# A fused relation layer with residual, one NeuronCore: one tile instead of four keeps its bias in the PSUM bank, and a new hand-written order of work

## Chip, cores, metric

One core of one Trainium2 chip. The metric is the device time of one execution in microseconds, the median of several executions; times inside an execution come from one profiled execution and count from the start of its span.

## Reference

For each of 4 sequences of 1024 rows with 512 columns, and a conditioning vector of 256 numbers per sequence (float32 throughout):

```python
hidden = jnp.concatenate([hidden0, hidden1], axis=-1)      # both are cond_512
x_mean = jnp.mean(x, axis=1, keepdims=True)
fused = jnp.concatenate([x, x_mean * ones_L, hidden[:, None, :] * ones_L], axis=-1)
relation = jax.nn.relu(jnp.einsum('bld,do->blo', fused, W) + b)
return x + relation
```

W is 1536 x 512. Its first 512 rows meet x, row by row; the rest gives one bias vector per sequence.

## The kernel before

**Work.** The 4096 rows are 32 tiles of 128 rows (8 per sequence). A tile's product is x (128 x 512) by W0 (512 x 512), in four slices j of the inner dimension, each as three matmuls on halves of the numbers: `hi` is the value rounded to the matmul's format, `lo` the rest, so x W0 = hi w_hi + lo w_hi + hi w_lo (`product`, L351 to L365; n = 0, 1, 2 in that order). That is 12 matmuls of 512 columns per tile, 396 in all with tile 31 done in two halves of 256 columns, so that its second half alone is late at the end.

**Names.** `X` loads x by rows (for the final sum, and for tiles 0 and 1 as the source of the transposes), `Z` loads it a second time, in 32-row quarters, for VectorE's transposes. `W` loads the four slices of W0; `wh`, `wl` make `w_hi`, `w_lo` (L209 to L221). `y0`, `y1` gather tiles 0 and 1 into a column order that TensorE transposes (`T0`, `T1`, L260); all later units (tiles 2 and 3, then four tiles each) are transposed by VectorE (L262). `h` makes `hi` on ACT and the column sums for the mean (L269), `l` makes `lo` (L275). `p5.2` is a block: the three products of tile 5, slice 2; `p0.1.2` a single product; `p31.1r` the three half products of tile 31's right half. For each sequence r, `as`, `c`, `m`, `f`, `fa`, `vh`, `vl` build the bias in the PSUM tile `acc`, the matmul `pb` (L339) spreads it over the rows, `bc` copies it to SBUF (L343). The eight PSUM banks are five for outputs (tile t in bank t mod 5), two for transposes, one for `acc`.

**Three ways out of a bank** (`WAYS`, one letter per tile):

```python
if WAYS[t] == "K":  # K{t}: o <- bank, ACT L428 or DVE L426;  b{t}: o <- o + bias, L432
...
else:               # "B", K{t}: o <- bank + bias, DVE only
    nc.vector.tensor_tensor(o, bank(t), biases[r], ALU.add)            # L436
...
nc.scalar.activation(o, o, AF.Relu)                                    # r{t}, L443
...
nc_of[e].tensor_tensor(x_tile(t), o, x_tile(t), ALU.add)               # F{t}, L450
...
# "I", P{t}: bank <- bias ahead of the products (ACT); F{t}: x <- max(bank, 0) + x
nc.scalar.activation(bank(t), biases[r], AF.Copy)                      # L415
nc.vector.scalar_tensor_tensor(x_tile(t), bank(t), 0.0, x_tile(t), ALU.max, ALU.add)  # L419
```

Tile 31, the last, is always "I" in two halves (L395, L399). `S` stores a finished tile from the place where its x lay.

**Order.** Nothing is scheduled by the program: `ORDER`, a list of some 550 names, is walked once and each name issues its instructions (L452 to L457). A suffix picks the engine (`@d` VectorE, `@a` ScalarE, `@p` GpSimd). So the list sets each engine's queue, and the DMA queue too: all transfers but the first go through SP, one after the other, and a store waits there for the sum that it stores. Every engine works its queue strictly in order.

Of the kernel before, what the change touches and what calls it, by code (L numbers as in the profile page):

```python
# [19 lines left out]
ORDER = """
W0@a X0.0 fill X0.1 relu fill W1 fill W2 fill fill W3 fill Z2.0 y0.0@d fill y0.1@d y0.2@d Z2.3 fill wh0r@a Z2.1
wh0l@d T0.2 T0.1 wl0l@d fill Z2.2 T0.0 y1.0@a y1.1@d T0.3 wl0r@p Z3.3 T1.2 h0.2 T1.0 T1.3 h0.0 l0.2@d h0.1 Z3.0
wh1@d p0.0.2 l0.0@d T1.1 p0.1.0 h1.1 Z3.2 wh2@d p0.0.1 h1.0 l1.1@d h1.2 p0.2.0 wl1@d p1.0.2 wh3@a p1.0.0 l0.1@d
p1.1.0 Z3.1 h1.3 l1.0@d p0.0.0 wl3@d h0.3 p1.1.1 p0.2.1 p1.3.0 wl2@p l1.2@d p0.1.2 l1.3@d p1.0.1 l0.3@d Z4.2 p0.3.2
p1.1.2 p0.1.1 p1.3.1 T2.2 p1.2.1 T2.0 p0.2.2 Z4.1 h2.2 p0.3.1 h2.0 p1.3.2 l2.2@d p1.2.2 l2.0@d p2.2 T2.3 Z4.3 T2.1
p3.0 h2.1 p1.2.0 h2.3 p2.0 l2.1@p Z4.0 K1@a l2.3@d p0.3.0 p3.2 K0@d C p3.1 B p2.3 V T3.2 M2 p3.3 T3.1 h3.2 p2.1 M0
h3.1 l3.2@d p4.2 T3.3 l3.1@p K2@a p5.2 T3.0 M1 h3.3 K3@d p7.2 h3.0 l3.3@p p7.1 l3.0@d M3 p4.0 to0 p5.0 T4.3 Z5.2
Z5.1 T4.0 p6.2 h4.3 Z5.3 t2 p4.3 T4.2 l4.3@p p4.1 t3 h4.2 T4.1 p6.1 h4.0 as0 l4.0@d p7.3 K4@a ac1@p Z5.0 t1 p5.3 t0  # L30
l4.2@d p5.1 ac0@d p8.3 Z7.3 c0.0 K5@a h4.1 p9.2 c0.1 p9.0 l4.1@p Z6.1 m0.0 p6.3 m0.1 p9.1 Z6.3 m0.2 p8.0 m0.3 p6.0
Z6.2 p8.2 K6@a Z6.0 f0 p8.1 fa0 p10.1 T5.1 Z7.1 vh0 p11.3 h5.1 vl0 p11.2 K8@a T5.0 Z7.0 l5.1@p p11.0 T5.2 pb0 p7.0
T5.3 bc0@a as1 p11.1 b1@p Z8.2 h5.2 c1.0 p10.2 Z8.0 h5.0 p10.3 c1.1 b0@p h5.3 p10.0 l5.2@d K7@a Z7.2 to1 p9.3 l5.0@d
K10@a l5.3@p m1.0 r0@a p12.1 X3.1 K9@a X0.2 p12.0 m1.1 b2@p K11@a p12.2 m1.2 X2.0 X1.1 p13.1 m1.3 b4@p r2@a p13.0
r1@a T6.3 f1 p15.3 b3@p T6.1 h6.3 p14.0 T6.2 h6.1 fa1 F1@p p14.2 h6.2 T6.0 p15.1 vh1 l6.2@d l6.1@p S1 h6.0 p14.3
X1.0 T7.2 p13.2 Z9.2 vl1 l6.3@p h7.2 Z8.1 p15.2 l6.0@d p14.1 Z8.3 T7.1 b6@p pb1 T7.0 p13.3 bc1@a b7@p p12.3 r6@a K14
Z9.0 p16.3 T7.3 F0@p r7@a K12 p15.0 h7.0 l7.2@d p16.1 h7.3 F2@p K13 p19.1 as2 p17.3 S0 h7.1 c2.0 l7.3@p X5.1 p16.2
r3@a Z9.3 K15 p16.0 Z9.1 to2 c2.1 b5@p p19.0 m2.0 X2.1 p17.1 m2.1 l7.1@p p18.0 m2.2 p20.3 b8@p m2.3 p19.3 l7.0@d f2
p20.2 F3@p r4@a fa2 p17.2 T8.0 vh2 p19.2 F7@p S3 h8.0 vl2 p18.2 r5@a T8.3 p17.0 F4@p T8.1 h8.3 p18.3 l8.0@d F6@p pb2
p20.1 bc2@a h8.1 p18.1 K16 F5@p S6 r8@a p20.0 K17 r14@a p21.1 T8.2 b9@p S5 T9.0 X3.0 p22.2 h8.2 S7 K18 p22.0 l8.1@p  # L40
r9@a S2 K20 X5.0 as3 p21.0 S4 K19 r18@a F14@p p22.1 X4.1 l8.2@d h9.0 X6.0 p22.3 c3.0 F8@p p25.0 X7.1 T9.1 p21.2 X6.1
T9.2 l8.3@p p21.3 h9.2 p23.2 K21 F9@p p25.1 X7.0 T9.3 r21@a S8 p24.1 c3.1 h9.3 b10@p X4.0 p23.1 S14 l9.0@d h9.1
p26.2 r13@a to3 F21@d r20@a p25.2 b11@p K22 p23.3 m3.0 p25.3 l9.1@p r11@a m3.1 p27.3 r22@a m3.2 r12@a p27.2 F11@p
m3.3 p27.0 F20@d f3 p23.0 S11 F13@p r10@a S20 fa3 p24.3 S21 vh3 p24.0 S9 F10@p S13 vl3 p24.2 l9.2@d p26.3 F12@p K23
pb3 p26.1 bc3@a l9.3@p S12 r17@a p27.1 K24 S10 P28 p26.0 K25 r23@a p28.0 F22@d r24@a F23@d p28.1 S22 r15@a K27 P29
S23 p28.2 F15@p P30 p28.3 P31r F18@d r27@a p29.0 S15 F17@p r16@a F28 S18 p29.2 r19@a p30.3 r25@a F19@d S17 p29.1
F16@p K26 S19 S28 p31.1r r26@a p29.3 F27@d S16 P31l p31.3r F25@d S27 p31.0r F24@p F29 p31.2r S25 p30.2 F31r S29
p30.1 F26@p S24 S31r p31.2l p30.0 S26 p31.1l F30 p31.3l p31.0l S30 F31l S31l
""".split()


# [433 lines left out]
```

## Time and profile before

| what | before |
|---|---|
| three executions, us | 101.2, 101.21, 102.0 (median 101.21) |
| the profiled execution, us | 101.09 |
| its span, us | 99.3 |
| busy share: TensorE, VectorE, GpSimd, ScalarE | 94%, 82%, 68%, 57% |
| granted TensorE clock | 1.00 of full speed throughout |
| moved by DMA | 27.88 MB, 281 GB/s over the span |

A row of the timeline is: start, time from the first start to the last end of the merged instructions, engine, line, operation, what it writes and reads, count, and in brackets the idle time of that engine before it and what ended it. PE is TensorE, DVE VectorE, ACT ScalarE, POOL GpSimd, SP the engine that issues the transfers. Successive instructions of an engine overlap a little, and matmuls overlap by almost half their length. A tile name's running number is left out (po is any of the five output banks).

### The profile page before, as it was taken

Reading aid. Unit: us, or ns where it says so; the run is one execution under the profiler, and the core shown is the slowest. Engines: PE = TensorE matmul, PEld = TensorE weight load, DVE = VectorE, ACT = ScalarE, POOL = GpSimd, SP = SyncE. Lnnn points to the kernel's source line nnn. Section 1 sums busy time; section 2 is a strip of 40 time slices with the busy share of each in tenths; the row PEclk is TensorE's granted clock in tenths of the full one; section 3 lists DMA queues with packets and bytes.
Section 4 is the critical chain, followed back from the end, with each engine's and each line's share of the span. In section 5 each row is a group of like instructions: output and inputs, shape, how many; then the busy total and the mean of one; then the engine's idle time right before and its main releaser. Section 6 shows DMA issues by size and latency. Waiting matters only on the chain.

```text
span 99.3 us, 1422 instructions
## 1 busy us (share of the span) xinstructions
PE 93.6 (94%) x417; PEld 75.3 (76%) x417; DVE 81.9 (82%) x139; ACT 56.7 (57%) x144; POOL 67.9 (68%) x67
## 2 busy tenths in 40 slices
...
GB/s 67 377 333 220 226 227 227 328 391 287 225 226 217 214 142 160 216 351 389 358 247 242 330 214 247 5 217 196 408 408 403 387 399 408 402 356 379 311 375 117
DMA packets 26433, 27.88 MB, mean 281 GB/s; under 512 B 1461, under 2 KB 17081, under 8 KB 26426
## 3 DMA queue, kind: packets, MB, share of 16 engines
...
q10 hardware_dynamic: 144, 0.26, 0.8%
...
## 4 chain that ended last, share of the span: by engine, by line
PE 90%; DMA 3%; DVE 2%; issue 0%
PE po L361 89%; DMA x<-in_L_cond_W_dram 3%; PE acc L339 1%; DVE o L236 1%; PE po L260 0%; DVE x L399 0%; DVE w_lo L221 0%; DVE w_hi L217 0%; PE acc L260 0%
## 5 line engine op out<-in xcount | busy, mean ns | idle before, releaser
L361 PE MATMUL po<-w_lo,hi 128*128 128x512 f32 (+1 forms) x132 | 50.5, 385 | 0.1
L361 PE MATMUL po<-w_hi,lo 128*128 128x512 f32 (+1 forms) x132 | 50.1, 383 | 0.0
L361 PE MATMUL po<-w_hi,hi 128*128 128x512 f32 (+1 forms) x132 | 50.0, 384 | 0.0
L275 POOL TENSOR_TENSOR lo<-xT,hi 128x512 fp32r<-128x512 f32 (+1 forms) x15 | 18.9, 1264 | 19.1 <-ACT hi L269 19.1
L361 PEld LDWEIGHTS po<-w_lo,hi 128*128 128x128 f32 x132 | 24.7, 188 | 5.5 <-issue 0.5
L450 POOL TENSOR_TENSOR x<-o,x 128x512 f32<-128x512 f32 x20 | 27.8, 1419 | 1.3 <-ACT o L443 1.3
L361 PEld LDWEIGHTS po<-w_hi,lo 128*128 128x128 f32 x132 | 24.8, 188 | 5.1
L361 PEld LDWEIGHTS po<-w_hi,hi 128*128 128x128 f32 x132 | 24.8, 188 | 5.1
L443 ACT ACTIVATE o<-o 128x512 f32<-128x512 f32 x28 | 16.5, 623 | 4.6 <-POOL o L432 3.0
L432 POOL TENSOR_TENSOR o<-o,bias 128x512 f32<-128x512 f32 x12 | 15.5, 1306 | 0.3 <-ACT bias L343 0.3
L269 ACT ACTIVATE hi<-px 128x512 fp32r<-128x512 f32 (+2 forms) x18 | 9.6, 534 | 7.1 <-DVE px L262 7.0
L315 DVE SCALAR_TENSOR_TENSOR acc<-w_mean,tot,acc 128x512 f32<-128x512 f32 x16 | 12.1, 754 | 0.6
L275 DVE TENSOR_TENSOR lo<-px,hi 128x512 fp32r<-128x512 f32 (+2 forms) x18 | 10.8, 606 | 1.4 <-ACT hi L269 1.4
L436 DVE TENSOR_TENSOR o<-po,bias 128x512 f32<-128x512 f32 x16 | 10.5, 677 | 1.5 <-PE po L361 0.8
L269 ACT ACTIVATE hi<-xT 128x512 fp32r<-128x512 f32 (+1 forms) x16 | 9.6, 598 | 3.1 <-DVE xT L262 3.0
L262 DVE STREAM_TRANSPOSE xT<-z 128x512 f32<-128x512 f32 (+1 forms) x16 | 10.3, 661 | 0.2
L262 DVE STREAM_TRANSPOSE px<-z 128x512 f32<-128x512 f32 (+1 forms) x16 | 10.3, 660 | 0.0
L428 ACT ACTIVATE o<-po 128x512 f32<-128x512 f32 x10 | 5.7, 598 | 6.3 <-PE po L361 6.3
L450 DVE TENSOR_TENSOR x<-o,x 128x512 f32<-128x512 f32 x8 | 8.4, 1074 | 0.4 <-ACT o L443 0.4
L301 DVE SCALAR_TENSOR_TENSOR acc<-wc,cT,acc 128x512 f32<-128x512 f32 x8 | 6.0, 748 | 0.9 <-ACT acc L296 0.6
L323 ACT ACTIVATE fold<-acc 64x512 f32<-64x512 f32 x4 | 2.4, 596 | 4.5 <-DVE acc L315 4.5
L221 POOL TENSOR_TENSOR w_lo<-x,w_hi 128x256 fp32r<-128x256 f32 (+1 forms) x2 | 2.1, 1064 | 4.1 <-ACT w_hi L215 2.8
...
## 6 DMA issues: line engine op xcount, KB each, us to landing
...
x<-in_x_dram SPq DMA_DIRECT2D x15, 512.0 KB, 6.6
...
```

The lines of the kernel that those rows point to most:

```text
L262: nc.vector.transpose(xT.rearrange("p (n q e) -> p n q e", q=Q // E, e=E), zs[z_of(u)][:, : n * NQ].rearrange("p n (q j e) -> p n j q e", ...
L269: nc.scalar.activation(his[buf][:, col : col + m], xT, AF.Copy, accum_out=sums[:, r, j, s : s + 1])
L275: nc_of[e].tensor_tensor(los[buf][:, col : col + m], xT, his[buf][:, col : col + m].bitcast(F32), ALU.subtract)
L301: nc.vector.scalar_tensor_tensor(acc, wc[:, k], cT[:, k, r : r + 1], acc, ALU.mult, ALU.add)
L315: nc.vector.scalar_tensor_tensor(acc, w_mean[:, j, :], tot[:, r, j : j + 1], acc, ALU.mult, ALU.add)
L323: nc.scalar.activation(fold, acc[high], AF.Copy)
L361: nc.tensor.matmul(v, lhsT=a[:, col : col + P], rhs=m, start=WAYS[t] != "I" and key not in done, stop=done.count(key) == 3 * J - 1, skip_g ...
L428: nc.scalar.activation(o, bank(t), AF.Copy)
L432: nc_of[e].tensor_tensor(o, o, biases[r], ALU.add)
L436: nc.vector.tensor_tensor(o, bank(t), biases[r], ALU.add)
L443: nc.scalar.activation(o, o, AF.Relu)
L450: nc_of[e].tensor_tensor(x_tile(t), o, x_tile(t), ALU.add)
```

## The change

Two tables change, no function. In `WAYS`, tiles 28 to 30 go from "I" to "B": the bias no longer sits in their bank ahead of the products but is added by VectorE on the way out, followed by a ReLU on ScalarE and a sum with x. `ORDER` is written anew nearly throughout.

```diff
-WAYS = "KKKKKKKKKKKKBBBBBBBBBBBBBBBBIIII"
+WAYS = "KKKKKKKKKKKKBBBBBBBBBBBBBBBBBBBI"
...
-wh0l@d T0.2 T0.1 wl0l@d fill Z2.2 T0.0 y1.0@a y1.1@d T0.3 wl0r@p Z3.3 T1.2 h0.2 T1.0 T1.3 h0.0 l0.2@d h0.1 Z3.0
+T0.1 y0.2@a fill Z2.3 wl0r@d h0.0 y1.0@d T0.2 Z3.1 h0.1 T0.3 wl0l@p l0.0@d p0.0.0 y1.1@a l0.1@d T1.0 T1.1 Z3.0
...
-p30.1 F26@p S24 S31r p31.2l p30.0 S26 p31.1l F30 p31.3l p31.0l S30 F31l S31l
+p31.1r S29 p31.3r F27@d r30@a p31.2r p31.0l S27 F31r p31.1l F30@d S31r p31.3l p31.2l S30 F31l S31l
```

TensorE's queue behind the warm-up matmuls. In these rows o12 and o11 hold the gathered tiles 0 and 1, po0 is the bank of tile 0, hi0 and lo0 its halves; before:

```order
L260 MATMUL px0_141<-ident_135,o12_117 128x128
L260 MATMUL po4_140<-ident_135,o12_117 128x128
L260 MATMUL po3_139<-ident_135,o11_116 128x128
L260 MATMUL acc_143<-ident_135,o11_116 128x128
L260 MATMUL po3_139<-ident_135,o11_116 128x128
L361 MATMUL po0_136<-w_lo_73,hi0_75 128x512
L260 MATMUL acc_143<-ident_135,o11_116 128x128
L361 MATMUL po0_136<-w_hi_72,hi0_75 128x512
L361 MATMUL po0_136<-w_hi_72,lo0_90 128x512
```

The same place after:

```order
L260 MATMUL po4_140<-ident_135,o12_117 128x128 x2
L361 MATMUL po0_136<-w_hi_72,hi0_75 128x512
L260 MATMUL acc_143<-ident_135,o11_116 128x128 x2
L361 MATMUL po0_136<-w_hi_72,lo0_90 128x512
L260 MATMUL po3_139<-ident_135,o11_116 128x128 x2
L361 MATMUL po0_136<-w_hi_72,lo0_90 128x512
L361 MATMUL po1_137<-w_hi_72,hi1_76 128x512
```

The first product of tile 0 stands ahead of tile 1's transposes, and the second between them; before, tile 1's transposes came first but for one.

VectorE's queue at its first loads (x2 holds tiles 0 and 1, x0 the slices of W0), before:

```order
L236 COPY o12_117<-x2_65 128x128 x2
L236 COPY o12_117<-x2_65 128x256
L217 CAST w_hi_72<-x0_63 128x256
L221 TENSOR_TENSOR w_lo_73<-x0_63,w_hi_72 128x256
L236 COPY o11_116<-x2_65 128x256
L275 TENSOR_TENSOR lo0_90<-po4_140,hi0_75 128x128
```

and after:

```order
L236 COPY o12_117<-x2_65 128x128
L217 CAST w_hi_72<-x0_63 128x256
L221 TENSOR_TENSOR w_lo_73<-x0_63,w_hi_72 128x256
L236 COPY o11_116<-x2_65 128x256
L275 TENSOR_TENSOR lo0_90<-px0_141,hi0_75 128x128
```

Two of tile 0's three copies went to ScalarE. The `w_lo` row is alike but is now the right half of W0's first slice, which waits for ScalarE's cast; the left half went to GpSimd (before, the other way round).

VectorE's queue at the end. Here po0 is the bank of tile 30, po4 of 29, po3 of 28, po2 of 27 and then of tile 31's right half, po1 of 31's left half; before:

```order
L450 TENSOR_TENSOR x0_63<-o6_111,x0_63 128x512
L436 TENSOR_TENSOR o0_105<-po1_137,bias3_121 128x512
L450 TENSOR_TENSOR x2_65<-o1_106,x2_65 128x512
L450 TENSOR_TENSOR x2_65<-o12_117,x2_65 128x512
L419 SCALAR_TENSOR_TENSOR x3_66<-po4_140,x3_66 128x512
L399 SCALAR_TENSOR_TENSOR x3_66<-po2_138,x3_66 128x256
L419 SCALAR_TENSOR_TENSOR x3_66<-po0_136,x3_66 128x512
L399 SCALAR_TENSOR_TENSOR x3_66<-po1_137,x3_66 128x256
```

and after:

```order
L436 TENSOR_TENSOR o2_107<-po3_139,bias3_121 128x512
L436 TENSOR_TENSOR o1_106<-po2_138,bias3_121 128x512
L436 TENSOR_TENSOR o3_108<-po4_140,bias3_121 128x512
L450 TENSOR_TENSOR x3_66<-o2_107,x3_66 128x512
L450 TENSOR_TENSOR x2_65<-o11_116,x2_65 128x512
L436 TENSOR_TENSOR o4_109<-po0_136,bias3_121 128x512
L450 TENSOR_TENSOR x2_65<-o1_106,x2_65 128x512
L399 SCALAR_TENSOR_TENSOR x3_66<-po2_138,x3_66 128x256
L450 TENSOR_TENSOR x3_66<-o4_109,x3_66 128x512
L399 SCALAR_TENSOR_TENSOR x3_66<-po1_137,x3_66 128x256
```

Tiles 28 to 30 now take two VectorE or GpSimd instructions each where they took one: an eviction with the bias, and a sum with both inputs in SBUF (tile 29's is on GpSimd).

## Rows read from the trace of the kernel before

**Rows 1.** The page's first part: busy us, share of span, instructions.
```profile
PE 93.6 (94%) x417; PEld 75.3 (76%) x417; DVE 81.9 (82%) x139; ACT 56.7 (57%) x144; POOL 67.9 (68%) x67
```

**Rows 2.** Chain that ended last, in order of time: start us, us, what.
```profile
9.80 25.97 PE po L361 x113
35.77 0.23 PE acc L339
...
49.14 13.60 PE po L361 x60
...
62.97 19.04 PE po L361 x84
...
95.37 0.42 DVE x L399
```

**Rows 3.** Timeline of the head, all engines.
```profile
4.18 0.42 ACT L215 ACTIVATE w_hi<-x 128x256 fp32r<-128x256 f32 x1 [1.34 <-DMA x<-in_L_cond_W_dram]
4.19 0.30 DVE L217 CAST w_hi<-x 128x256 fp32r<-128x256 f32 x1 [0.28 <-DMA x<-in_L_cond_W_dram]
...
4.68 0.84 POOL L221 TENSOR_TENSOR w_lo<-x,w_hi 128x256 fp32r<-128x256 f32 x1 [2.79 <-ACT w_hi L215]
...
4.86 0.42 ACT L234 ACTIVATE o<-x 128x256 f32<-128x256 f32 x1 [0.26 <-DMA x<-in_x_dram]
4.86 0.81 DVE L236 COPY o<-x 128x256 f32<-128x256 f32 x1
5.18 0.26 ACT L269 ACTIVATE hi<-po 128x128 fp32r<-128x128 f32 x1
5.33 0.19 ACT L269 ACTIVATION_READ_ACCUMULATOR hi<-po 128x1 f32 x1
...
5.60 0.28 DVE L275 TENSOR_TENSOR lo<-po,hi 128x128 fp32r<-128x128 f32 x1
...
5.73 0.33 PE L260 MATMUL po<-ident,o 128*128 128x128 f32 x1 [0.68 <-DVE o L236]
...
5.80 0.41 DVE L217 CAST w_hi<-x 128x512 fp32r<-128x512 f32 x1
...
6.82 1.29 POOL L221 TENSOR_TENSOR w_lo<-x,w_hi 128x512 fp32r<-128x512 f32 x1 [1.29 <-DVE w_hi L217]
...
8.98 0.67 DVE L221 TENSOR_TENSOR w_lo<-x,w_hi 128x512 fp32r<-128x512 f32 x1
...
10.33 0.86 PE L361 MATMUL po<-w_hi,lo 128*128 128x512 f32 x3
```

**Rows 4.** VectorE's instructions by line and form: busy us, mean ns.
```profile
L436 DVE TENSOR_TENSOR o<-po,bias 128x512 f32<-128x512 f32 x16 | 10.5, 677 | 1.5 <-PE po L361 0.8 <-ACT bias L343 0.7
...
L262 DVE STREAM_TRANSPOSE px<-z 128x512 f32<-128x512 f32 x14 | 9.5, 694 | 0.0
...
L450 DVE TENSOR_TENSOR x<-o,x 128x512 f32<-128x512 f32 x8 | 8.4, 1074 | 0.4 <-ACT o L443 0.4
...
L419 DVE SCALAR_TENSOR_TENSOR x<-po,x 128x512 f32<-128x512 f32 x3 | 2.0, 682 | 0.9 <-PE po L361 0.9
```

**Rows 5.** VectorE's busy time (second number) in one stretch.
```profile
61.35:95.80 34.45, 30.45 (x44) 1.00 0.90 330
```

**Rows 6.** Timelines of VectorE and GpSimd.
```profile
37.30 1.55 DVE L301 SCALAR_TENSOR_TENSOR acc<-wc,cT,acc 128x512 f32<-128x512 f32 x2 [0.32 <-ACT acc L296]
...
84.11 1.31 DVE L450 TENSOR_TENSOR x<-o,x 128x512 f32<-128x512 f32 x2
...
85.94 1.45 DVE L450 TENSOR_TENSOR x<-o,x 128x512 f32<-128x512 f32 x1
...
89.62 2.89 DVE L450 TENSOR_TENSOR x<-o,x 128x512 f32<-128x512 f32 x2
...
85.55 8.12 POOL L450 TENSOR_TENSOR x<-o,x 128x512 f32<-128x512 f32 x5 [1.29 <-ACT o L443]
```

**Rows 7.** The page's DMA issues: count, KB each, median us to landing.
```profile
x<-in_x_dram SPq DMA_DIRECT2D x15, 512.0 KB, 6.6
```

More of the change, by code (lines that the diff above doesn't have):

```diff
@@ L15 @@
 PSUM = bass.MemoryType.PSUM
-WAYS = "KKKKKKKKKKKKBBBBBBBBBBBBBBBBIIII"
+WAYS = "KKKKKKKKKKKKBBBBBBBBBBBBBBBBBBBI"
 ORDER = """
-W0@a X0.0 fill X0.1 relu fill W1 fill W2 fill fill W3 fill Z2.0 y0.0@d fill y0.1@d y0.2@d Z2.3 fill wh0r@a Z2.1
-wh0l@d T0.2 T0.1 wl0l@d fill Z2.2 T0.0 y1.0@a y1.1@d T0.3 wl0r@p Z3.3 T1.2 h0.2 T1.0 T1.3 h0.0 l0.2@d h0.1 Z3.0
-wh1@d p0.0.2 l0.0@d T1.1 p0.1.0 h1.1 Z3.2 wh2@d p0.0.1 h1.0 l1.1@d h1.2 p0.2.0 wl1@d p1.0.2 wh3@a p1.0.0 l0.1@d
-p1.1.0 Z3.1 h1.3 l1.0@d p0.0.0 wl3@d h0.3 p1.1.1 p0.2.1 p1.3.0 wl2@p l1.2@d p0.1.2 l1.3@d p1.0.1 l0.3@d Z4.2 p0.3.2
@@ L27 @@
[L27 to L46, printed above, removed]
@@ L47 @@
-F16@p K26 S19 S28 p31.1r r26@a p29.3 F27@d S16 P31l p31.3r F25@d S27 p31.0r F24@p F29 p31.2r S25 p30.2 F31r S29
-p30.1 F26@p S24 S31r p31.2l p30.0 S26 p31.1l F30 p31.3l p31.0l S30 F31l S31l
+W0@a X0.0 fill X0.1 relu fill W1 fill W2 fill fill W3 fill Z2.2 y0.0@d y0.1@a fill Z2.0 fill wh0l@d wh0r@a Z2.1 T0.0
+T0.1 y0.2@a fill Z2.3 wl0r@d h0.0 y1.0@d T0.2 Z3.1 h0.1 T0.3 wl0l@p l0.0@d p0.0.0 y1.1@a l0.1@d T1.0 T1.1 Z3.0
+p0.0.1 wh1@d h1.0 T1.2 T1.3 h0.3 p0.1.1 l1.0@d wl1@p Z3.3 h1.1 p1.0.0 h1.2 p1.0.2 l1.1@d p0.0.2 wh2@a l1.2@d p0.1.0
@@ new lines @@
+p1.1.0 wh3@d h1.3 p1.0.1 Z3.2 h0.2 wl2@d p1.2.0 p1.2.1 p0.3.0 wl3@p l1.3@d p1.2.2 l0.2@d p1.3.0 l0.3@d Z4.3 p0.1.2
+p1.1.1 p1.1.2 p0.3.1 T2.2 p0.2.1 p0.2.2 Z4.0 T2.3 h2.2 p0.2.0 T2.1 p1.3.2 l2.2@d p0.3.2 h2.1 p1.3.1 T2.0 p3.2 h2.3
+Z4.2 h2.0 l2.3@d p2.2 l2.1@p K1@a K0@d p3.3 B l2.0@d Z4.1 p3.0 C p2.0 V p3.1 T3.2 M1 p2.1 T3.3 h3.2 p2.3 M0 h3.3
+l3.2@d p6.2 T3.1 l3.3@p M2 K2@d p4.2 h3.1 T3.0 p5.2 l3.1@p M3 h3.0 p4.3 Z5.1 K3@a l3.0@d p6.3 as0 Z5.3 T4.3 p4.1
+Z5.0 T4.0 h4.3 p4.0 T4.2 h4.0 l4.3@p p6.0 t3 t1 p5.1 T4.1 to0 t0 p6.1 h4.1 K4@d p7.2 h4.2 t2 Z5.2 ac1@p K6@a l4.2@d
@@ new lines @@
+p7.3 ac0@d p5.0 l4.1@p Z6.0 c0.0 p7.0 c0.1 p7.1 Z6.2 m0.0 p11.3 K7@a p8.3 m0.1 Z6.1 p5.3 m0.2 p9.3 Z6.3 m0.3 p8.2
+l4.0@d f0 p9.1 Z7.0 K5@a fa0 p11.1 T5.3 vh0 X0.2 p11.0 vl0 h5.3 Z7.3 p10.0 T5.2 l5.3@p Z7.2 p11.2 T5.0 pb0 T5.1 p9.0
+Z7.1 bc0@a as1 p9.2 b2@p h5.1 c1.0 p12.3 X3.1 h5.0 p10.3 c1.1 b5@p h5.2 X1.0 p10.2 l5.0@d r2@a l5.1@p p10.1 T6.3
+l5.2@d p8.0 h6.3 X1.1 to1 T6.0 p8.1 Z8.1 b1@p T6.1 p12.0 K8@a m1.0 K10@a p12.1 b3@p m1.1 h6.1 p15.1 K11@a T6.2 p13.2
+b0@p h6.0 m1.2 Z9.3 p13.1 K9@a Z8.2 m1.3 r1@a l6.1@p p15.3 r3@a l6.0@d p13.3 f1 Z8.3 l6.3@p p14.2 h6.2 fa1 p14.0
```

12 lines of the change are left out of this document (added).

## Prediction

> **What bounds the kernel now.** I read the page's first part, then the chain that ended last, then the timeline of the head, the rows by form of VectorE and GpSimd, and the timeline of the end. TensorE is busy for 94% of the span, no other engine over 82% [rows 1]. The chain says what that means: from 9.80 us it is TensorE alone, product after product with only the four bias matmuls between them, to 95.35, then one VectorE add, and the end [rows 2]. In steady state a product of 512 columns starts every 13.60 / 60 = 0.2267 us, a block (three products, a `p` entry with two numbers) takes 0.680 us, and the stretches leave no room for a stall (84 products: 19.04). So only three things can move the time: the head, in which TensorE waits for transposes, weights and halves; a stall put where there is none; and the 3.5 us behind the last add at 95.37 + 0.42 = 95.79, which are a store, its landing and the program's end. Span 99.3, own time of this execution 101.09, so 1.8 us lie around it; the sum is made against 101.09, which is 0.1 under the median of 101.21.
>
> **The head.** Before, TensorE transposes tile 0, sits idle 0.68 us until 5.73 for the copy `y1.1` that feeds tile 1's transposes, and then does products with further pauses; the 14th product starts at 9.80 (113 products lie between there and the first bias matmul, and 126 precede it by the order), the 16th at 10.33 [rows 2, 3]. After, step by step, durations from [rows 3]. `w_hi` of W0 can't come earlier (its right half is cast 4.18 to 4.60, when the load has landed). ACT copies `y0.2` behind it until 4.92, then makes the first `hi` (0.26 from 4.84, with the 0.19 for the accumulator done 5.2: the same overlaps as at 5.18 and 5.33). So `p0.0.0` fits into the old idle stretch, one product for nothing. On VectorE `w_lo` of W0's right half now stands ahead of `y1.0`, ready at 4.64, while GpSimd takes the left half at 4.57 (0.08 behind its cast, as before) for 0.84, to 5.41. Before, a VectorE copy that ran beside such an instruction (0.84 from 4.68, to 5.52) took 0.81 and ended 0.15 behind it. I let VectorE wait likewise: `w_lo` ends 5.70, `y1.0` 5.92, tile 1's transposes begin at 5.98, 0.25 later than before. `p0.0.1` then needs a `lo` (0.28) and starts at 6.2; two transposes; `p0.1.1`, the third product, needs the cast of W1 (0.41, to 6.65) and starts at 6.70. From there each product's inputs are ahead of it: the closest is `w_lo` of W2. VectorE makes three `lo` until 7.8, waits with the cast of W3 for GpSimd's `w_lo` of W1 (1.29 from 6.73, to 8.02) until 8.3, and needs 0.67 more, to 8.9, for the 13th product at 6.70 + 10 x 0.2267 = 8.97. The 16th starts at 6.70 + 13 x 0.2267 = 9.65: **0.68 us earlier**. Bounds: if VectorE's `w_lo` isn't held at 4.64, only `y1.0` behind it is, to 5.41 + 0.15 = 5.56, 0.36 earlier, and the gain is 1.04; if `w_lo` of W2 falls behind GpSimd's `w_lo` of W3 (1.29), the 13th product comes 0.55 later and the gain is 0.13.
>
> **The middle.** The entries between the bias matmuls become 57, 20, 19, 29 and 23 (58, 19, 20, 28, 23 before). The first bias matmul therefore falls at 35.77 - 0.68 (the head) - 0.68 (one block fewer) = 34.41, the others at 34.41 + 0.23 + 20 x 0.68 = 48.24, 61.39 and 81.34, and TensorE would end at 95.35 - 0.68 = 94.67, the last add at 95.1. Loads: W keeps its place, the Z loads change places within their unit (a transpose needs all four quarters of it anyway), and the bytes are the same; I cost that at nothing, since the eight blocks of tiles 2 and 3 (5.4 us) stand between the loads of tiles 4 to 7 and their first product. Without that cover a late load counts in full. One load is moved far: X7.1 (tiles 30 and 31) is now queued on SP behind the stores of tiles 11, 14, 19 and 13, and so waits for GpSimd's add of tile 13: two instructions of 1.3 us behind the last bias matmul, 84.0. With 6.6 to land [rows 7] it is there near 91, some 3 us before the first add that needs it; each us beyond that is a us on the end.
>
> **VectorE at the end.** Tiles 28 to 30 lose three ACT fills of the bank and three VectorE adds out of the bank (0.68), and gain three VectorE evictions with the bias (0.68), three ReLUs on ACT and three adds. Over the program VectorE now does twelve of the SBUF adds of L450 and GpSimd nineteen, before eight [rows 4] and twenty. ACT's sum is even, and at 57% it has room [rows 1]. VectorE's isn't. From the end of its last piece for the third bias (61.35) to 95.80 it was busy 30.45 of 34.45 us [rows 5]. After, that stretch has one transpose less (0.69), three evictions more (2.03), three adds from the bank less (2.05) and four L450 adds more. What one of these costs is what matters. Alone it takes under 0.7 (the two at 84.11 need 1.31 together, and GpSimd starts its next at 85.55). Beside a GpSimd add it takes 1.45 (at 85.94) and 2.89 for two (at 89.62); the mean of eight is 1.07 [rows 4, 6]. In the new order GpSimd has five instructions left when the last bias is made and then one, the add of tile 29; so of the last four VectorE adds I take three at 0.69 and the one of tile 27, which meets tile 29's, at the mean: 3.14. Busy: 30.45 - 0.69 + 2.03 - 2.05 + 3.14 = 32.88.
> When can it start? VectorE takes up the second bias 1.53 us after the first bias matmul (37.30 against 35.77 [rows 2, 6]), needs 24.05 us from there to 61.35, and one transpose more (0.69): 34.41 + 1.53 + 24.05 + 0.69 = 60.68. It must still wait for four things at TensorE's new dates, each the date of a block counted from the bias matmuls above less the end of what VectorE has ahead of it: the third bias (0.35), tile 17's last product (0.35), tile 21's (the 15th block behind 61.62, out at 72.0; VectorE free at 71.3: 0.70), tile 24's (0.40). That is 1.8, and the last add ends at 60.68 + 32.88 + 1.80 = **95.4**, 0.3 behind what TensorE alone would allow and 0.4 ahead of before. With the 3.5 us behind it: 101.09 - 0.4 = **100.7**. Bounds: all four adds alone, 95.0, is no bound any more (TensorE's 95.1 is); three of the four at 1.45 costs 1.9 more, of which the wait for tile 24 (0.40) absorbs a part: 96.9.
>
> The Trainium skill speaks against this part of the change: its page "SBUF — State Buffer", section "Who interferes with whom", says that a VectorE instruction with two SBUF inputs and a GpSimd instruction that reads SBUF exclude one another, the one that issues first keeping the shared ports for its whole length. By that rule the trace agrees: the add at 85.94, issued 0.39 behind a GpSimd add, took 1.45 [rows 6]. Where the rule strikes at three of the four added sums, the sum comes to 102.2, rival B below, against 100.7 by the mean of the rows.
>
> **Rivals.**
> A. The head gives its most: `w_lo` isn't held up at 4.64, and VectorE is late nowhere. For it: 4 us of idle VectorE in the last stretch before. Against: the copy of 0.81. TensorE gains 1.04, the last add follows it: 101.09 - 1.04 = 100.05.
> B. VectorE becomes the bound. Mechanism: at the end its adds and GpSimd's take turns; tile 27's eviction comes late, so tile 31's bias reaches its bank late and TensorE waits for it, and the last five VectorE instructions queue. Price 96.9 - 95.79 = 1.1 slower: 102.2. It decides when more than 0.4 us is lost there beyond my sum, which is one collision of 1.45 - 0.69 = 0.76. For it: five GpSimd instructions stand beside adds of tiles 23, 20, 25 and 26, and the page's rule; against: the mean of 1.07 already includes such meetings.
> C. The head gives nothing, `w_lo` of W2 behind that of W3: gain 0.13, all of VectorE's dates 0.55 later, 95.95: 101.2. For it: the margin of 0.07. Against: VectorE reaches its instruction without a semaphore in between, GpSimd only after one.
>
> **How the numbers follow.** My forecast 0.52, A 0.15, B 0.17, C 0.16. A measurement of this kernel tells about 1% (1.0 us) from no change. Under 100.2 lie most of A and a small part of mine: 0.18. Over 102.2 lie a good half of B and a little of C: 0.13. The rest, 0.69, is within 1%. The range leaves out about a tenth on either side: 100.0 to 102.1.
>
> **What would show it.** Right: the first product before tile 1's transposes near 5.2; the 16th product near 9.65; bias matmuls near 34.4, 48.2, 61.4 and 81.3; the last VectorE add near 95.4, behind other VectorE work and not behind a wait for TensorE. Wrong: a product chain broken between 10 and 81 us; a VectorE wait on the X7.1 load; tile 31's products waiting for ACT's bias; or tile 1's transposes after 6.2.

## The result, and the profile after

The changed kernel takes 102.46 us (median of 20 runs, 101.62 to 103.84) where the kernel before takes 101.69 on the same chips (20 runs, 101.03 to 102.30): ratio **1.0067, 95% interval 1.0040 to 1.0093**. The forecast was 100.7, between 100.0 and 102.1; half a microsecond of the distance is the base, 101.21 in the three executions of the forecast and 101.69 here. Ratios leave out the executions that are more than 1.5% above the fastest of their kernel. The profiled execution took 101.62, span 99.7; it is the fastest of its 20, which matters below. The kernel before was profiled at 101.09, also near its fastest.

The page's first part after, to be held against [rows 1]: VectorE is up from 81.9 to 84.9 us.

```profile
PE 94.4 (95%) x417; PEld 75.6 (76%) x417; DVE 84.9 (85%) x141; ACT 56.9 (57%) x145; POOL 68.2 (68%) x67
```

The chain that ended last, by engine (the page), and three of its pieces in order of time (start us, us, what):

```profile
POOL 38%; DVE 29%; DMA 10%; issue 7%; ACT 6%; SPq 5%; DVEq 1%; POOLq 0%; ACTq 0%
```

```profile
5.21 4.02 DMA z<-in_x_dram
...
31.73 0.61 ACT fold L323
...
33.09 0.59 ACT v_acc L331
```

The reader should stop here. Before, the chain was TensorE alone from 9.80 to 95.35 [rows 2]. Now TensorE isn't in it at all: the chain goes through GpSimd, VectorE and loads. TensorE is still busy 95% of the span. That several engines have become late together, so that a delay in any of them reaches the end, is my reading of the chain; the runs below test parts of it.

The head (TensorE; VectorE; GpSimd), against [rows 3]:

```profile
5.50 0.62 PE L361 MATMUL po<-w_hi,hi 128*128 128x512 f32 x1
5.95 0.43 PE L260 MATMUL acc<-ident,o 128*128 128x128 f32 x2
...
9.88 0.40 PE L361 MATMUL po<-w_hi,lo 128*128 128x512 f32 x1
```

```profile
4.30 0.29 DVE L217 CAST w_hi<-x 128x256 fp32r<-128x256 f32 x1 [0.50 <-DMA x<-in_L_cond_W_dram]
4.75 0.94 DVE L221 TENSOR_TENSOR w_lo<-x,w_hi 128x256 fp32r<-128x256 f32 x1 [0.15 <-ACT w_hi L215]
```

```profile
4.68 0.72 POOL L221 TENSOR_TENSOR w_lo<-x,w_hi 128x256 fp32r<-128x256 f32 x1 [2.78 <-DVE w_hi L217]
```

The first product stands ahead of tile 1's transposes, and the 16th starts at 9.88: 0.45 us earlier than before, where 0.68 was forecast. The first load's second half landed 0.1 later, and VectorE's `w_lo` beside GpSimd's ended at 5.69, as forecast (5.70). The third product started at 6.67 (forecast 6.70); the 0.23 that is missing lies behind it, where the next thirteen products took 3.21 us instead of 2.95.

The four bias matmuls start 1.09, 0.23, 0.91 and 0.20 us earlier than before (34.51, 48.52, 61.67 and 81.64 in the timeline, 35.60, 48.75, 62.58 and 81.84 in that of before; the chain of [rows 2] dates them 0.17 later). The forecast had 1.36, 0.67, 1.35 and 0.67. VectorE's windows row and its rows by form, against [rows 5] and [rows 4]:

```profile
61.44:96.08 34.64, 33.92 (x160) 28.07 (x158) 32.89 (x47) 20.80 (x44) 28.80 (x23) 1.00 0.99 341
```

```profile
L450 DVE TENSOR_TENSOR x<-o,x 128x512 f32<-128x512 f32 x12 | 11.7, 998 | 0.1
```

VectorE is busy 32.89 us (fourth column of the row) and idle 1.75 between the end of its part of the third bias and the last add: the forecast had 32.88 and 1.80. But that stretch begins at 61.44, not at 60.68, and so the last add ends at 96.08 instead of 95.4. The end, VectorE, then SP:

```profile
93.03 0.68 DVE L436 TENSOR_TENSOR o<-po,bias 128x512 f32<-128x512 f32 x1
93.63 1.19 DVE L450 TENSOR_TENSOR x<-o,x 128x512 f32<-128x512 f32 x1
94.74 0.41 DVE L399 SCALAR_TENSOR_TENSOR x<-po,x 128x256 f32<-128x256 f32 x1
95.08 0.68 DVE L450 TENSOR_TENSOR x<-o,x 128x512 f32<-128x512 f32 x1
95.67 0.41 DVE L399 SCALAR_TENSOR_TENSOR x<-po,x 128x256 f32<-128x256 f32 x1
```

```profile
95.27 1.46 SPq L145 DMA_DIRECT2D out_dram<-x  x3
```

No row of VectorE has a bracket: nothing is waited for, VectorE runs without a gap to the end, while the last product started at 95.15. Before, the last add waited for TensorE. On SP three stores follow one another until 96.73, so the last is issued at 96.33, 0.25 behind its add; before, at 95.83 behind 95.80. What the DMA engines did (last two numbers: their share of time, GB/s), the kernel before and then after:

```profile
78.00:84.00 6.00, 6.00 (x28) 4.95 (x27) 5.03 (x8) 3.44 (x7) 6.00 (x5) 1.00 1.06 399
84.00:88.00 4.00, 4.00 (x20) 3.34 (x19) 3.99 (x6) 4.00 (x9) 2.71 (x3) 1.00 1.04 398
...
92.00:98.00 6.00, 3.34 (x21) 2.79 (x19) 2.56 (x5) 0.00 (x0) 1.67 (x1) 1.00 0.88 322
```

```profile
78.00:84.00 6.00, 6.00 (x28) 4.97 (x27) 5.72 (x8) 2.87 (x5) 6.00 (x5) 1.00 0.85 271
84.00:88.00 4.00, 4.00 (x20) 3.30 (x19) 3.90 (x6) 1.45 (x3) 4.00 (x4) 1.00 1.02 319
...
92.00:98.00 6.00, 3.36 (x26) 2.93 (x24) 4.08 (x7) 1.70 (x4) 1.39 (x1) 1.00 0.99 368
```

From 78 to 88 us the new order moves (399 - 271) x 6 + (398 - 319) x 4 = 1.08 MB less. SP's queue had stood: the stores of tiles 5 and 6, ready since 63.1 and 69.5, are issued at 75.9 and 77.1 behind those of tiles 12 and 15; X7.0, which may not overwrite tile 5 before that is stored, is issued at 79.9 (73.7 before); and X7.1 and the store of tile 22 stand behind the wait for GpSimd's add of tile 13 (84.3). From 84 to 88 the engines are busy again (1.02) and still move less, which a standing queue doesn't explain. They are then full to the end.

### The profile page after: what moved, and what is told of

The parts are those of the page before. It is cut to its first block, busy times and chain, and to the rows that moved or that the text cites. A ratio compares the mean times of both kernels' runs of the same rounds, so it can differ in the third digit from the quotient of the medians.

```text
span 99.7 us, 1421 instructions
## 1 busy us (share of the span) xinstructions
PE 94.4 (95%) x417; PEld 75.6 (76%) x417; DVE 84.9 (85%) x141; ACT 56.9 (57%) x145; POOL 68.2 (68%) x67
## 4 chain that ended last, share of the span: by engine, by line
POOL 38%; DVE 29%; DMA 10%; issue 7%; ACT 6%; SPq 5%; DVEq 1%; POOLq 0%; ACTq 0%
POOL o L432 15%; POOL x L450 13%; POOL lo L275 9%; DVE acc L315 6%; DVE x L450 6%; SPq L145 5%; DMA out_dram<-x 4%; DMA z<-in_x_dram 4%; ACT hi L269 4%; DVE o L436 3%; DVE px L262 3%; DVE xT L262 3%; DVE lo L275 3%; DMA bias<-in_cond_dram 2%; DVE acc L301 2%
## 5 line engine op out<-in xcount | busy, mean ns | idle before, releaser
L361 PE MATMUL po<-w_hi,hi 128*128 128x512 f32 (+1 forms) x132 | 51.0, 387 | 0.1
L450 POOL TENSOR_TENSOR x<-o,x 128x512 f32<-128x512 f32 x19 | 26.0, 1400 | 3.9 <-ACT o L443 3.9
L443 ACT ACTIVATE o<-o 128x512 f32<-128x512 f32 x31 | 18.5, 624 | 6.3 <-DVE o L436 6.2
L436 DVE TENSOR_TENSOR o<-po,bias 128x512 f32<-128x512 f32 x19 | 12.4, 679 | 1.0 <-PE po L361 1.0
L450 DVE TENSOR_TENSOR x<-o,x 128x512 f32<-128x512 f32 x12 | 11.7, 998 | 0.1
L221 POOL TENSOR_TENSOR w_lo<-x,w_hi 128x512 fp32r<-128x512 f32 (+1 forms) x3 | 3.7, 1231 | 4.6 <-DVE w_hi L217 4.6
```

The lines of the kernel that those rows point to most:

```text
L361: nc.tensor.matmul(v, lhsT=a[:, col : col + P], rhs=m, start=WAYS[t] != "I" and key not in done, stop=done.count(key) == 3 * J - 1, skip_g ...
```

## The experiments

Each ratio is to the kernel before, in the same batch of runs. Eight of the eighteen runs (e1, e2, e4, e6, e7, e9, e11, e15) came out above every range that was named for them beforehand. A cut is the order of one kernel up to a named entry and from there the entries of the other that are left, in its order.

**Which part costs?** Four runs: the ways undone, the head undone, the head alone, VectorE relieved.

```diff
# e1_ways_undone, on the changed kernel: tiles 28 to 30 as "I"
-WAYS = "KKKKKKKKKKKKBBBBBBBBBBBBBBBBBBBI"
+WAYS = "KKKKKKKKKKKKBBBBBBBBBBBBBBBBIIII"
-K28 r28@a F28@d (29, 30 likewise)
+P28 (early, behind bc3@a; 29 behind K25, 30 behind r25@a), F28 in the place of K28
```


> The changed kernel with tiles 28 to 30 back to the bias in the bank (three ACT fills, three VectorE adds out of the bank; their evictions, ReLUs and SBUF adds gone), order else as changed. If VectorE's queue at the end makes the change slow: VectorE loses two SBUF adds and GpSimd one, tile 27's eviction and with it tile 31's bias come in time, the last VectorE add ends right behind TensorE near 95.5 (96.08 changed), 0.5 us less than the changed kernel: ratio to before 0.998 to 1.003. If the loss sits ahead of the last bias matmul (late loads, VectorE's waits in the middle): as the changed kernel, 1.004 to 1.009.

Measured 1.0127 (1.0101 to 1.0153). VectorE was relieved: its last add waits 1.01 us for TensorE. It became slower all the same: four stores follow one another, and the last is issued at 97.00, 0.72 us behind the last add (VectorE, then SP):

```profile
95.85 0.42 DVE L399 SCALAR_TENSOR_TENSOR x<-po,x 128x256 f32<-128x256 f32 x1 [1.01 <-PE po L361]
```

```profile
94.96 2.44 SPq L145 DMA_DIRECT2D out_dram<-x  x4
```

The theory that VectorE's added work alone makes the loss fell.

```diff
# e2_head_before: the kernel before up to p0.3.0, then the changed kernel
# e3_head_alone: the changed kernel up to p1.3.1, then the kernel before, its ways
```


> The order of before up to the last product of tiles 0 and 1, then the rest of the changed order. If the new head gains and the rest loses: TensorE 0.4 us later from the first bias matmul on, and VectorE's dates with it: ratio to before 1.009 to 1.013. If VectorE's end doesn't depend on the head (waits in between absorb it) or the new head gives nothing: 1.004 to 1.008.

> The changed order up to the last product of tiles 0 and 1, then the rest of before, ways of before. If the 0.45 us that the 16th product gained come through to the end: last VectorE add near 95.35, ratio to before 0.994 to 0.998. If something behind the head (a load, a VectorE date) takes them back: 0.999 to 1.003.

Measured 1.0189 (1.0164 to 1.0213, four executions) and **0.994 (0.9918 to 0.9962)**. The new head gives 0.6% on the old rest, and its removal costs the changed kernel 1.2%. In e3's profiled execution the 16th product is 0.45 earlier than before but the last add only 0.14 (95.66): TensorE pauses for 0.31 in all between 12.6 and 13.4. The loss of the changed kernel is in the rest of the new order.

```diff
# e4_two_to_pool, on the changed kernel
-F24@d F26@d
+F24@p F26@p behind F17@p; F27@d ahead of K30; S26 behind S17
```


> The changed kernel with the adds of tiles 24 and 26 moved from VectorE to GpSimd's idle stretch (88.9 to 92.9), and tile 27's add ahead of tile 30's eviction. If VectorE's queue is the bound at the end: its evictions of 28, 27, 29 come 0.6 us earlier, TensorE doesn't wait for tile 31's bias, the last add ends near 95.5: 0.5 us less than the changed kernel, ratio to before 0.998 to 1.003. If the loss sits ahead of the last bias matmul: 1.004 to 1.009.

Measured 1.0138 (1.0097 to 1.0180). As a relief it failed: GpSimd's add of tile 26 met VectorE's of tile 28 (1.24 us), its add of tile 29 that of tile 27 (1.78), and the last add ended 0.94 later behind the last product than TensorE asks for. It tells only that here the work moved to GpSimd came back as longer adds on VectorE.

**Where does it arise, and do the transfers matter?**

```diff
# e5_stores_early, on the changed kernel, SP alone
-S4 X5.0 X4.0 S9 X6.1 S8 X6.0 S12 S5 S15 S6 S21 S18 X7.0 S11 S14 S19 S13 X7.1 S22 S20 S23
+S4 S5 X5.0 X4.0 S6 S9 X6.1 S8 X6.0 X7.0 X7.1 S12 S15 S21 S18 S11 S14 S19 S22 S13 S23 S20
# e6_stores_held, on the kernel before, SP alone
-X6.0 X7.1 X6.1 X7.0 S8 X4.0 S14 S11 S20 S21 S9 S13 S12
+X6.0 X6.1 X4.0 S11 S13 S12 X7.0 X7.1 S8 S14 S20 S21 S9
```


> The changed kernel with nothing but the order of its transfers on SP altered: the stores of tiles 5 and 6 right behind their adds (63, 69.5 us) instead of at 76 to 77 us, both halves of the loads into the seventh group of x (X7.0, X7.1) right behind X6.0 instead of at 79.9 and 84.7, the store of tile 22 ahead of the wait for GpSimd's add of tile 13 (84.3). All other engines keep every instruction. Theory 1 (the changed kernel loses because its DMA engines run at 240 to 300 GB/s from 78 to 88 us and the stores then drain late): these bytes move before 84, the stretch from 88 on is shorter by 0.3 to 0.5 MB, and the loss goes: ratio to the kernel before 0.993 to 1.000. Rival 2 (the loss is in what the engines do after 62 us, VectorE and TensorE): as the changed kernel, 1.004 to 1.009. Rival 3 (traffic beside the products slows VectorE and GpSimd): above 1.009.

> The converse on the kernel before: every engine but SP as it was, X7.0, X7.1 and the stores of tiles 8, 14, 20, 21 and 9 held back behind the store of tile 12 (83 us), so that SP issues only three of the usual ten transfers from 73 to 83 us. Theory 1: the DMA engines stand half empty for some 3 us before 83, about 1.1 MB is left for the end, and the kernel before becomes slower by 0.5 to 1.3 per cent. Rival 2: the last store is issued as before and lands 2.4 us later, ratio 0.998 to 1.003, unless the products' adds wait for X7 (tile 28's add at 88.4 would have to be late in the trace).

Measured 1.0042 (1.0012 to 1.0073) and **1.0486 (1.0448 to 1.0524)**. The first took off a quarter of a per cent, with intervals that overlap, and lies in the range that was named for the rival (1.004 to 1.009). The second is nearly four times the upper end of what was expected, with the products almost where they were (last add at 96.05, before 95.80). Its DMA engines, and SP near the end:

```profile
78.00:84.00 6.00, 6.00 (x28) 4.99 (x27) 4.97 (x8) 3.39 (x7) 6.00 (x5) 1.00 0.25 94
...
92.00:98.00 6.00, 3.58 (x22) 2.99 (x20) 3.92 (x6) 0.11 (x1) 1.42 (x1) 1.00 1.05 405
```

```profile
94.77 5.74 SPq L145 DMA_DIRECT2D out_dram<-x  x9
```

At 94 GB/s from 78 to 84, 1.8 MB are left for later; from 88 on the engines are full at 400 to 405. Nine stores, two of them halves, are issued back to back in 5.74 us. The last nine issues took 0.33 to 0.41 each before; here the first seven take 0.59 to 0.61 and start 0.69 apart, close to the 0.66 that 256 KB need at 400 GB/s. I read it as SP held to the pace at which the bytes leave. The last store is issued 4.03 us behind the last add. So the time behind the last add is a quantity that the order sets.

```diff
# e7_after_to_62: the changed kernel up to bc2@a, then the kernel before, its ways
# e8_after_to_82: the changed kernel up to bc3@a, then the kernel before, its ways
```


> Place of the loss: the changed kernel's order up to the third bias pair's matmul and its copy (62 us), then the rest of the kernel before in its order, with the ways of the kernel before (tiles 28 to 30 have their bias in the bank). Theory 1, and rival 2 too, put the loss behind this point: 0.990 to 0.996, as with the new head alone (0.994). If the loss is made between 11 and 62 us (rival 4: the new middle loses the head's gain): 1.000 to 1.010.

> Place of the loss, second cut: the changed kernel's order up to the fourth bias pair (82 us), then the rest of the kernel before, and its ways. SP's order up to X7.0 is that of the changed kernel, X7.1 comes ahead of the wait for tile 13. Theory 1: most of the delay in the transfers is already there: 1.003 to 1.010. Rival 2 in the form that the last 20 us lose (four added adds, tile 27 late): 0.990 to 0.997.

Measured 1.0229 (1.0180 to 1.0278) and 0.9944 (0.9911 to 0.9978). The first says nothing of the place: the join itself broke the chain of products (VectorE idle 2.3 us near 68). The second, whose runs scatter from 100.44 to 104.07 (median of all twelve 101.45, beside 101.72: 0.997), points to a loss of about 1% behind 82 us, which is most of it.

```diff
# e9_k27_ahead, on the changed kernel
-K26 p29.3 r25@a r26@a F25@d p29.1 F26@d p28.1 S25 F16@p S26 p29.2 K28 p29.0 K27
+K26 K27 p29.3 r25@a r26@a F25@d p29.1 F26@d p28.1 S25 F16@p S26 p29.2 K28 p29.0
# e10_ways_k27_stores: e1 + the move of e9 + the SP order of e5
# e11_after_to_35: the changed kernel up to bc0@a, then the kernel before, its ways
```


> The changed kernel with one instruction moved on VectorE: the eviction of tile 27 (90.63 to 91.31) ahead of the adds of tiles 25 and 26, so that it ends near 88.4 and the bias copy into tile 31's bank (91.88) can start about 0.6 us earlier. The 0.23 us stall of TensorE at 91.84 should be gone. If VectorE, gapless from 83.5 to 96.08 in the changed kernel, is the bound at the end, the last add still ends near 96.1 relative to the same landings (14.4 us behind the fourth bias matmul) and the ratio to the kernel before stays at 1.004 to 1.009. If TensorE's stall is what is lost at the end, the last add comes 0.2 us earlier and the ratio falls to 1.001 to 1.006.

> Three edits on the changed kernel at once: tiles 28 to 30 keep their bias in the bank as before, the eviction of tile 27 stands ahead of the adds of tiles 25 and 26, and the transfers are in the order of the run with stores early. Theory now (the changed kernel loses at the end only, through three things that mask each other: TensorE's stall at tile 31's bank, VectorE gapless to the end, stores and the load X7.1 bunched behind 84 us): from the fourth bias matmul to the end of the span 17.3 to 17.6 us as in the kernel before (17.45), where the changed kernel has 18.06, and a ratio of 0.996 to 1.002. If a part of the loss sits in the middle of the new order (before 82 us): 1.003 to 1.008, with the stretch behind the fourth bias matmul still at 17.5.

> Third cut: the changed kernel's order up to the first bias pair (35 us), then the rest of the kernel before and its ways. If the new middle from 35 us on loses nothing, this is as the cut at 82 us (median 101.45 of 12 runs beside 101.72, 0.994 to 0.998). If the gain of the head is lost between 11 and 35 us, where TensorE waits for landings of z: 0.998 to 1.004. With the new head alone (cut at 11 us) it was 0.994.

Measured 1.0102 (1.0056 to 1.0149), 1.0046 (1.0018 to 1.0075) and 1.0139 (1.0097 to 1.0181). In e9 the last add did come 0.17 nearer to the fourth bias matmul (14.27 against 14.44), and the ratio gained nothing. Its end on VectorE and SP shows why:

```profile
95.45 0.41 DVE L399 SCALAR_TENSOR_TENSOR x<-po,x 128x256 f32<-128x256 f32 x1
```

```profile
94.74 2.46 SPq L145 DMA_DIRECT2D out_dram<-x  x4
```

The last add ends at 95.86; four stores take 2.46 us to issue, and the last starts 0.95 behind the add. e10 has all three relieved in part, still 0.60 between its last add and its last store, and 17.92 us from the fourth bias matmul to the end of the span (before 17.45). e11 broke the chain at its join (TensorE idle 1.2 us at 40.5) and tells nothing.

**Transfers ordered to the end.** SP's order as in e5, and besides S10, S16 and S17 ahead of S25 and S26, S28 ahead of S24 (their adds are done at 81.8, 87.7, 89.0; 89.5 and 90.1; 92.5 and 93.1).

```diff
# e12_transfers, on the changed kernel, SP alone (from S13 on)
-S13 X7.1 S22 S20 S23 S25 S26 S16 S10 S17 S24 S28 S29 S27 S31r S30 S31l
+S13 S10 S23 S20 S16 S17 S25 S26 S28 S24 S29 S27 S31r S30 S31l
# e13_transfers_k27: e12 + the move of e9
# e14_transfers_k27_ways: e13 + the ways of e1
# e16_transfers_ways: e12 + the ways of e1
# e15_stores_on_act, on the changed kernel: S27@a S31r@a S30@a
```


> The changed kernel with nothing but SP's order altered, now to its end: as in the run with stores early, and besides the stores of tiles 10, 16 and 17 (adds done at 81.8, 87.7, 89.0) ahead of the stores of tiles 25 and 26 (89.5, 90.1), and that of tile 28 ahead of tile 24's. Stores theory (the last stores are bunched, SP issues them at the DMA engines' pace of 0.65 to 0.7 us each, and the last one starts late): 0.75 MB leave before 90 instead of behind it, the last store is issued within 0.1 us of the last add, the span ends 3.4 to 3.5 us behind the last add, and the ratio falls to 0.998 to 1.003 (changed kernel 1.0067, stores early alone 1.0042). If VectorE's end sets it: 1.004 to 1.008.

> As the run before, and the eviction of tile 27 ahead of the adds of tiles 25 and 26 (TensorE's stall at tile 31's bank shorter by 0.1 to 0.2 us; the last add 0.1 to 0.2 us nearer to the fourth bias matmul, as 14.27 beside 14.44 us in the run with that edit alone). Stores theory: 0.997 to 1.001. If the stores do not matter: 1.003 to 1.010.

> As the run before, and tiles 28 to 30 keep their bias in the bank as in the kernel before. The last add then waits for TensorE alone (13.94 us behind the fourth bias matmul in the run with ways, eviction and stores early), and with the stores flowing the span ends 3.4 us behind it: 17.3 to 17.4 us behind the fourth bias matmul, as in the kernel before (17.45). Ratio 0.995 to 1.000. If it is above 1.002 with that stretch at 17.4, the rest of the loss sits ahead of 82 us.

> The changed order with the transfers in the order of the runs with all transfers moved, and tiles 28 to 30 with their bias in the bank as before; the eviction of tile 27 stays behind the adds of tiles 25 and 26. Transfers alone gave 1.0028, with the eviction 0.9975, with both 0.988. If the ways act by VectorE's share at the end, they give here what they gave there, about 1 per cent: 0.990 to 0.996, with TensorE's stall of 0.23 us at tile 31's bank still in the trace. If they act only together with the eviction: 1.000 to 1.005.

> The changed kernel with the last stores of tiles 27 and 30 and the right half of 31 issued by ScalarE, which is idle behind 94.4 us, instead of by SP. If SP's issuing is the limit at the end, the last store is issued at once behind the last add and the ratio falls by 0.2 to 0.6 per cent from 1.0067. If the DMA engines' pace is the limit, the bytes in front of the last store are the same, it lands when it did, and the ratio stays within 0.2 per cent of 1.0067.

| tile 27's eviction, ways | SP's order of the change | transfers ordered to the end |
|---|---|---|
| as changed | 1.0067 (1.0040 to 1.0093) | 1.0028 (0.9996 to 1.0060) |
| eviction ahead | 1.0102 (1.0056 to 1.0149) | 0.9975 (0.9945 to 1.0005) |
| ways undone | 1.0127 (1.0101 to 1.0153) | 0.9945 (0.9925 to 0.9966) |
| both | not run; 1.0046 (1.0018 to 1.0075) with the order of e5 | **0.988 (0.9832 to 0.9928)**; again, as e18, 0.9901 (0.9872 to 0.9931) |

This table is the main finding. In the left column neither edit helps; in the right column, where only SP's order differs, both do, and within the intervals they add up. Undoing the ways is worth 0.7 to 1% there (1.0028 to 0.9945, 0.9975 to 0.988 or 0.9901); the eviction alone is worth 0.5%, with intervals that just overlap. The traces show the place for the two edits: from the last add to the end of the span it is 4.29 us in e9 and 3.47 in e13, 4.70 in e1 and 2.77 in e16, pairs in which SP's order alone differs. Between the changed kernel and e12 it is 3.62 and 3.48, less than the ratios differ by. e14's end:

```profile
92.00:98.00 6.00, 2.98 (x25) 2.78 (x23) 2.14 (x4) 0.00 (x0) 0.00 (x0) 1.00 0.68 250
```

```profile
95.02 0.42 DVE L399 SCALAR_TENSOR_TENSOR x<-po,x 128x256 f32<-128x256 f32 x1 [1.01 <-PE po L361]
```

```profile
95.47 0.33 SPq L145 DMA_DIRECT2D out_dram<-x  x1
```

The bracket is back: the last add waits for TensorE. Its store is issued 0.03 behind it, with the one ahead of it out at 94.87, into engines that are 68% busy, takes 0.33 to issue, lands in 1.7 us, and the span ends 2.76 us behind the last add.

e15 measured 1.0238 (1.0194 to 1.0282) and doesn't answer its question. SP's store of tile 24, whose add was done near 94.1, was issued at 97.99; the waits view of 88 to 100 us charges SP with it:

```profile
SPq L145 <- DMA out_dram<-x: 5.0, 2, 4.7
```

SP stood 4.7 us for a landing of another store. The trace's semaphores tell which: tile 24's store reports its landing on the same semaphore as ScalarE's first store, that of tile 27, issued at 95.80, and SP's wait ended when that one landed, at 97.92. So the wait came from a semaphore that two queues share in this program. Why the program shares it isn't settled, and whether ScalarE's issuing would have helped without it isn't either.

**What scatters the changed order?** Unit 3 of z is tiles 4 to 7, and Z3.2 is the quarter of it that is loaded last. In the traces of the changed order, VectorE resumes when it lands, and the first bias matmul follows by nearly the same time wherever that is. Three executions of the new order up to there, the changed kernel, e1 and e16 (VectorE's transpose, TensorE's bias matmul, of each):

```profile
14.84 0.73 DVE L262 STREAM_TRANSPOSE px<-z 128x512 f32<-128x512 f32 x1 [1.29 <-DMA bias<-in_cond_dram]
...
34.51 0.45 PE L339 MATMUL acc<-v_acc,ones 128*128 128x512 f32 x1
```

```profile
15.22 0.73 DVE L262 STREAM_TRANSPOSE px<-z 128x512 f32<-128x512 f32 x1 [1.47 <-DMA z<-in_x_dram]
...
34.85 0.44 PE L339 MATMUL acc<-v_acc,ones 128*128 128x512 f32 x1
```

```profile
15.84 0.73 DVE L262 STREAM_TRANSPOSE px<-z 128x512 f32<-128x512 f32 x1 [1.50 <-DMA z<-in_x_dram]
...
35.43 0.48 PE L339 MATMUL acc<-v_acc,ones 128*128 128x512 f32 x1
```

19.67, 19.63 and 19.59 us apart; the first row's releaser is misnamed, since Z3.2 landed at 14.71, 0.13 ahead of it as in the others. In twelve such traces the transpose starts between 14.59 and 15.91 (the middle two 14.84 and 14.95), and the distance is 19.59 to 19.94 (left out: e17, below, and e7, e8 and e12, with 15.64 to 16.29 and 19.61 to 20.34). The kernel before, and e3, have room there: VectorE waits 1.5 us for the fold ahead of its first bias. 0.6 of that is the fold itself; the other 0.9 is room, for VectorE's sum is ready at 31.45, and ScalarE makes the fold from 32.35, behind a copy that waits for TensorE. VectorE before, ScalarE before, VectorE after:

```profile
32.97 0.69 DVE L327 TENSOR_TENSOR acc<-acc,fold 64x512 f32<-64x512 f32 x1 [1.53 <-ACT fold L323]
```

```profile
32.35 0.59 ACT L323 ACTIVATE fold<-acc 64x512 f32<-64x512 f32 x1
```

```profile
32.37 0.69 DVE L327 TENSOR_TENSOR acc<-acc,fold 64x512 f32<-64x512 f32 x1
```

In e3 the quarter landed at 15.41, and TensorE had no pause between 13.4 and its first bias matmul. So with the old middle this late load is absorbed, and in the traces with the new one the bias matmul moves with the landing by its full amount. From the first bias matmul to the fourth it makes no further difference: 47.10 to 47.20 us in thirteen of the fifteen traces that have the new middle as far as that (46.93 was forecast; in the other two, e8 and e12, TensorE stands another 0.9 ahead of the third). No run moved the load itself. Two last runs test VectorE's part, by taking one copy off it in that stretch:

```diff
# e18_again: e14 once more
# e17_k2_on_act, on e14
-K2@d
+K2@a
```


> The kernel of transfers, eviction and ways together once more, as the base of the next run and for the size of its gain: 0.984 to 0.993. Its first bias matmul 19.6 to 19.7 us behind VectorE's transpose that waits for the last quarter of z's third-but-one unit (unit 3).

> That kernel with one copy (tile 2 out of its bank, 0.69 us on VectorE at 17.6) made by ScalarE, which is idle there for 0.76 us. If VectorE's chain from the landing of unit 3 to the first bias sets TensorE's date, the first bias matmul follows the transpose by 19.1 to 19.4 us instead of 19.6, and the ratio is 0.1 to 0.5 per cent below that of the base in the same runs. If TensorE's own products set it, the difference stays at 19.6 or TensorE has no stall there, and the ratio is that of the base within 0.15 per cent.

Measured 0.9901 (0.9872 to 0.9931) and **0.9851 (0.9818 to 0.9884)**, medians 100.70 and 100.23 in six runs each. The distance fell from 19.85 to 19.41. The difference is what was expected at its upper end, but the intervals overlap, e14 had given 0.988 for the base, and the base's distance was 19.66 there: likely, not certain. e17 has the lowest ratio of this study and beats the kernel before and the changed one, by 1.5% and, through their ratios, 2.1%.

## Why the prediction was wrong

- **Where the miss lies.** The profiled execution took 101.62 where 100.7 was forecast: of the 0.92, 0.68 are there at the last add (96.08 for 95.4), 0.12 come behind it (3.62 for 3.5), and 0.12 lie outside the span (1.92 for 1.8).
- **The head: right mechanism, size off.** 0.45 us in the profile instead of 0.68, within its bounds (0.13 to 1.04); alone it is worth 0.6%.
- **VectorE's sum: right.** Busy 32.88 forecast, 32.89 measured; the four added adds 3.14 and 3.23; waits 1.80 and 1.75. Of the four, three took 0.68; tile 27's, which met GpSimd's add of tile 29, took 1.19. So the forecast's mean came nearer than the reading by which three of four collide (rival B's price). Collisions hit other adds: tiles 20 and 25, 1.77 and 1.66, both begun while a GpSimd instruction ran, as the Trainium skill ("SBUF — State Buffer", "Who interferes with whom") has it: the one that issues second is blocked for the whole of the other. The page says what a meeting does, and the order says who meets.
- **First failed step: "I cost that at nothing", of the loads.** The cover named was the eight blocks of tiles 2 and 3 between the loads of tiles 4 to 7 and their first product. The load was the right one, tiles 4 to 7, but the reader that counted wasn't TensorE: it was VectorE, whose transposes of these tiles stand in its chain to the first bias. The forecast moved that bias up by 1.36 us (two times 0.68) without asking whether VectorE could have it ready: of the 1.53 of idle time ahead of its fold 0.9 was the allowance, and the move used it up. In the profiled execution the load landed near the middle of its range (14.71), and the price beyond the 0.23 that the head fell short is small: the bias matmuls miss their forecast by 0.27, 0.44, 0.44 and 0.47 (stalls of 0.1 at 33.0 and 41.6, a smaller one at the first bias matmul). And VectorE misses by 0.76 the date at which VectorE's last stretch begins (61.44 for 60.68; 0.37 of it is a wait at 58.1 for another load, Z8.0). In other traces of this order the first bias matmul is up to 1 us later still (35.53 in e5).
- **Second failed step: "the 3.5 us behind the last add", taken as a constant, and a rearranged SP queue costed by one load alone.** I did follow X7.1 (forecast there near 91, landed 89.0, first needed at 94.7) and stopped there. What counted were the bytes: 1.08 MB less moved from 78 to 88 us, and a queue of stores at the end. From the last add to the end of the span the runs show 2.76 (e14), 3.50 (before), 3.62 (after), 4.29 (e9), 4.70 (e1), 4.79 (e2) and 8.64 us (e6). In the profiled execution of the changed kernel that is only 0.12 too much; in e2's, whose kernel has the same end in the same order, it is 1.29. Reordering SP alone, with every other engine's program kept, took the ratio from 1.0067 to 1.0028, with the eviction from 1.0102 to 0.9975, and with the ways from 1.0127 to 0.9945.
- **Rival B: right in part.** VectorE did become the bound, gapless from 83.5 to 96.08, and tile 31's bias did come late: a product started 0.46 behind the one ahead of it at 92.30 where 0.23 is the pace. It took no extra collisions. But it wasn't the only bound, and undoing the ways paid only when the stores flowed; there it paid 0.7 to 1%, where the forecast had put VectorE 0.3 us behind TensorE. The median (102.46) lies near rival B's price (102.2), which is luck: the mechanism behind it is late loads and three limits at the end, not one.
- The profiled execution alone (101.62) would have made the error look half as large; its first bias matmul was 0.34 earlier than e1's under the same order.

What stays open: how much of the median's 0.8 us above the profiled execution is the loads' landing and how much the stores, since no ordinary execution of the changed kernel was traced. The traces of other kernels with its order allow either: a first bias matmul up to 1 us later, and 0.7 to 1.2 us more behind the last add (e9, e2). The joins of e7 and e11 broke the order, so no run isolates the stretch from 35 to 62 us; the traces put its price at 0.2 us (47.1 for 46.93).
